# Layer norm of the next element: its sums by accumulating transfers instead of matmuls, and begun one stage earlier

## The chip, the cores and the metric

The kernel runs on one core of a Trainium2 chip. The metric is the device time of one execution in microseconds (us). One execution was also taken by the hardware profiler; its trace gives start and duration of every instruction, and tells for each idle stretch of an engine what ended it. The engines are TensorE (PE in the profile; PEld is its weight load), VectorE (DVE), ScalarE (ACT), GpSimd (POOL) and SyncE (SP). Here POOL and SP mostly issue transfers (DMAs). A time such as 1149.31 is us from the start of the span.

## The reference

Two layers are applied to x of 8 elements, 512 channels and 32 x 32 positions (1024 tokens), all in float32. Layer 0 normalises each token over its channels, runs attention with eight heads of 64 channels, projects, and adds its input. Layer 1 normalises groups of 16 channels, runs attention with one head over all 512 channels, projects, and adds its input.

```
# layer 0, S = 1024 tokens, C = 512
mu = mean(x_flat, axis=-1);  var = mean((x_flat - mu)**2, axis=-1)
xn = (x_flat - mu) * rsqrt(var + 1e-5) * gamma + beta
q, k, v = xn @ Wq.T + bq, xn @ Wk.T + bk, xn @ Wv.T + bv      # 8 heads
out = softmax(q k^T / 8) v;   x1 = out @ Wo.T + bo + x_flat
# layer 1
h = group_norm(x1, 32 groups)
q, k, v = wq h + bq, wk h + bk, wv h + bv
o = softmax(q^T k / sqrt(512)) v;   y = x1 + wp o + bp
```

## The kernel before, in words

x is kept with channels on the partitions. A block `x_b_jk` (128 x 1024 numbers) holds 256 channels j of 512 tokens k, as two chunks of 128 channels side by side; four blocks are one element. The projections and layer 1's two large products are done by the class `Product`: 2 x 2 blocks with seven block products instead of eight. Each product is one `step`, and `STEPS` names which of three PSUM tiles x, y and z it writes. After a step ScalarE copies a PSUM tile away (`copy`) or VectorE adds such a copy and another PSUM tile to make an output (`out`, line 343). A later step that writes the same PSUM tile waits for this. A unit is seven steps, and there are two or four units to a project.

The program goes through the elements in order. For element b the stages are: values and queries of layer 0 (`v`, `q`), eight pairs of heads (`Pair`: scores at line 683, exponential at 686, values at 701), keys of element b+1, output project and group norm, then layer 1: `qa`, scores `s1`, values `vm`, and the last product `o1` (`Whole.values`), whose outputs y are scaled by the inverse of the sums (line 905), get a bias and layer 1's input (line 906) and are stored (line 907). The input of layer 1 was put away in DRAM (`x1_away`) and comes back as `x1r` (line 904), one load to an output. After `o1` come values and queries of element b+1, and in them the layer norm of element b+2. The four blocks of x for it are loaded there.

The instructions of TensorE, VectorE, ScalarE and POOL stand in the order in which the program makes them (`manual_schedule`). Small pieces of other work wait in the list `side`. `tick`, called in each step between the matmuls and the copy, takes the next piece (two where `pieces` is 2) and puts its instructions there. An engine works through its list in order, so an instruction that waits holds all behind it. SyncE's loads and stores are not in this written order: a scheduler places them by when it believes them ready. On SyncE's queue too a transfer that waits, for instance a store whose output isn't there, holds those behind it.

The layer norm of the next element is such a chain of pieces (`LayerNorm.steps`), queued after the third step of the first `v` unit (`LN_AT`). VectorE adds the four channel chunks of x (lines 524 and 528, tile `lns`). TensorE adds over the 128 partitions with a matrix of 1/512 (line 519): the mean, to PSUM, two matmuls for the two halves of the tokens, each of which the trace records as two. ScalarE copies the mean to both halves of the partitions (line 537), VectorE centres x (543), ScalarE squares it (547), the squares are added (tile `lnq`) and summed over partitions by TensorE in the same way. `root` takes the variance from PSUM with a transpose (491), makes its inverse root, copies it to the partitions and expands it (496); then x is scaled (571) and gets gamma and beta (575).

The sums of the exponentials take another way already. `halve` is an accumulating transfer on POOL's queue that adds the upper 64 partitions of a tile to the lower ones; `fold` adds the remaining two times 32 partitions and lays half a row of tokens on each group of 32 partitions of a small tile; VectorE transposes and reduces this (lines 720, 721). So a sum over partitions is made without TensorE. Groups of two pairs are folded together (`PairSums`), after the values of the first of them. Layer 1's sums go the same way in `Whole.fold`, and `Whole.inverse` uses them during the second step of `o1`; ScalarE spreads the inverse with eight small copies (878) and VectorE expands it.

Of the kernel before, what the change touches and what calls it, by code (L numbers as in the profile page):

```python
# [19 lines left out]
P = 128  # L20
EPS = 1e-5
NUM_GROUPS = 32
HEADS = 8
LN_AT = 3

# [41 lines left out]
def fast_path(ctx: ExitStack, tc: tile.TileContext, x: bass.AP, vecs: dict, weights: dict, out: bass.AP,  # L67
# [244 lines left out]
    def later(*work):  # L312
        side.extend(work)
# [180 lines left out]
    def expand(t, r):  # L494

        nc.vector.transpose(t.rearrange("p (k i) -> p k i", i=BL), r.unsqueeze(2).to_broadcast((P, r.shape[1], BL)))  # L496

    def inverse_root(r, var, name):

        t = small.tile(list(r.shape), F32, tag=f"{name}_t", name=f"{name}_t")  # L500
        nc.scalar.activation(t, var, AF.Ln, bias=eps)
        nc.scalar.activation(r, t, AF.Exp, scale=-0.5)

        def refine():
            nc.vector.scalar_tensor_tensor(t, var, EPS, r, ALU.add, ALU.mult)
            nc.vector.scalar_tensor_tensor(t, t, -0.5, r, ALU.mult, ALU.mult)
            nc.vector.scalar_tensor_tensor(r, t, 1.5, r, ALU.add, ALU.mult)
        return refine

    class LayerNorm:  # L510


        def __init__(self, b, xt):
            self.b, self.xt = b, xt

# [15 lines left out]
        def mean(self):  # L531
            ps = bank(f"mean_{self.b}")
            self.over_channels(ps)
            self.mu = big_tile(f"mu_{self.b}")
            for k in range(NH):
                for r in range(2):
                    nc.scalar.copy(self.mu[ts(r, D), ts(k, HB)], ps[ts(k, D), :])

        def rows(self, t, k):
# [37 lines left out]
        def steps(self):  # L577

            self.sq = {}
            for k in range(NH):  # L580
                yield from self.add("lns", k, self.xt[0, k], self.xt[1, k])
            yield
            self.mean()
            yield
            yield
            blocks = ((0, 0), (1, 0), (0, 1), (1, 1))
# [9 lines left out]
            yield from self.add("lnq", 1, self.sq[0, 1], self.sq[1, 1])  # L596
            yield
            self.variance()
            yield
            yield from self.root()  # L600
            for n in range(4):
# [107 lines left out]

    def fold(f, q, t, cols):  # L710

        for n in range(2):
            nc.gpsimd.dma_start(out=f[ts(q, BL), :], in_=t[ts(n, BL), cols], accum_op=ALU.add if n else ALU.bypass)  # L713

    def halve(t):
        nc.gpsimd.dma_start(out=t[:D, :], in_=t[D:, :], accum_op=ALU.add)  # L716

    def folded_sums(d, t, f):

        nc.vector.transpose(t, f)  # L720
        nc.vector.tensor_reduce(d, t.rearrange("p (k i) -> p k i", i=BL), mybir.AxisListType.X, ALU.add)

    class PairSums:


        def __init__(self, two):
            self.two, self.tag = two, two[0].tag
            self.r = small.tile([P, HB // BL], F32, tag="r", name=f"r_{self.tag}")
            self.rr = [small.tile([P, HB // BL], F32, tag=f"rr{n}", name=f"rr_{p.tag}") for n, p in enumerate(two)]

        def fold(self):

            self.f = half_tile(f"fold_{self.tag}")
            for pair in self.two:
                halve(pair.sum)
            for n, pair in enumerate(self.two):
                for i in range(2):
                    fold(self.f, 2 * n + i, pair.sum, ts(i, HB))

# [53 lines left out]
    class Whole:  # L793
# [61 lines left out]
        def fold(self):  # L855
            self.f = half_tile(f"fold1_{self.b}")
            for hf in range(NH):
                halve(self.total[hf])
            for a in range(2):
                for hf in range(NH):  # L860
                    fold(self.f, 2 * a + hf, self.total[hf], ts(a, HB))

        def inverse(self):
# [4 lines left out]
            def invert():  # L868
                d = small.tile([P, HB // BL], F32, tag="d", name=f"d1_{b}")
                folded_sums(d, half_tile(f"fold1t_{b}"), self.f)  # L870
                nc.vector.tensor_copy(both[:D, :], d[D:, :])
                nc.vector.tensor_add(both[:D, :], both[:D, :], d[:D, :])
                invert_sums(r[:D, :], both[:D, :])
# [60 lines left out]
    with tc.manual_schedule(engines=ORDERED):  # L934
        nq = natural(wq, "q1")
        nk = natural(wk, "k1")
        ln = LayerNorm(0, x_next)
        pieces = ln.steps()
# [36 lines left out]
        for n, w in (("v", wv_now), ("q", wq_now), ("o", wo), ("a", wa), ("m", wm)):  # L975
            complete_later(n, w)
        later(*(lambda c=c: score_bias(c) for c in range(NC)))
        units, kt = project("k0", wk_now, bias_of("bk0"), hb)
        for u in units:
# [3 lines left out]

        def next_values_and_queries(b, wv, wq):

            xt = load_x(b + 1) if b + 1 < B else None
            units, v = project_v(f"v{b}", wv, hb)
            units[0].step(LN_AT)
            ln = None
            if xt:  # L990
                ln = LayerNorm(b + 1, xt)
                ln.queue()
# [3 lines left out]
            for u in units:  # L996
                u.pieces = 2
            units[0].rest()
            return ln, v, q, units[1]

        ln, vts, qt, q_last = next_values_and_queries(0, wv_now, wq_now)
        for b in range(B):
            more = b + 1 < B
            stats = small.tile([P, NC, NH, 6], F32, tag="stats", name=f"stats_{b}")
            ot = {"tag": f"o_{b}"}
            first = Pair(b, 0, 0, qt, kt, vts, ot)
            first.scores(range(NM))
            q_last.rest()
            pairs = [first] + [Pair(b, hf, c, qt, kt, vts, ot) for hf in range(NH) for c in range(NC) if hf + c > 0]
            for i, p in enumerate(pairs):  # L1010
                if i + 1 < len(pairs):
                    pairs[i + 1].scores(range(NM))
                if i < 2 and more:
# [6 lines left out]
                if i == 7 and more:  # L1020
                    hb = operands(ln.result())
                    add_operands(hb)
                p.values(scaled=(p is pairs[-1]))
                if i % 2 == 0:
                    sums = PairSums(pairs[i : i + 2])
                    if i + 2 < len(pairs):
                        sums.fold()
                    else:
                        sums.product()
                        later(sums.invert, sums.copies, lambda: sums.rows(1), lambda: sums.rows(0),  # L1030
                              lambda: sums.scale(0))
                elif i + 1 < len(pairs):
                    at_scores.append(sums.invert_folded)
# [49 lines left out]
            if more:  # L1083
                wv_next, wq_next = load_w("v", b + 1), load_w("q", b + 1)
            o_units = whole.values(vm)
            check = iter(()) if more else all_checks()
            o_units[0].step(1)
            whole.inverse()
            o_units[0].step(1)
            next(check, None)  # L1090
            o_units[1].step(2)
            next(check, None)
            for u in o_units:
                u.rest()
            until(lambda: not side)
            if more:
                kt = {ik: block(f"k{b + 1}_again_{ik[0]}{ik[1]}") for ik in kn_away}
                for ik, d in kn_away.items():
                    nc.sync.dma_start(out=wide(kt[ik]), in_=d)
                ln, vts, qt, q_last = next_values_and_queries(b + 1, wv_next, wq_next)  # L1100

# [383 lines left out]
```

## Time and profile before

Three runs took 2935.98, 2937.20 and 2937.74 us, median 2937.2.

| what | us |
|---|---|
| the profiled execution's own time | 2937.39 |
| its span, first to last instruction | 2935.6 |
| TensorE busy | 2914.7 |
| VectorE busy | 1788.5 |
| ScalarE busy | 1044.1 |
| POOL busy | 238.5 |
| share of TensorE in the chain that ended last | 98% |
| granted clock of TensorE, mean | 0.997 |
| busy share of the 16 DMA engines, queue of SyncE | 20.4% |
| the same, queue of POOL | 7.7% |

A group's row gives line, engine and operation, the tiles it writes and reads, shapes and count, then busy time, mean ns of one, and the engine's idle time before it with what ended it. In a timeline a row is: start, us, engine, line, operation, tiles, shapes, count, and idle time before in brackets. Rows of one tile overlap on TensorE, since a matmul starts before the one before has ended; what an instruction costs there is the distance of the starts. A row of transfers ends with the size of one and the median us from issue to landing.

One element takes 358.3 us from its mark to the next one's. In the element that the prediction follows, layer 1's last product `o1` runs from 1104.62 to 1152.69, the values of the next element to 1178.07, its queries to about 1191.6.

### The profile page before, as it was taken

How to read it: one execution, taken by the hardware profiler on the slowest of the kernel's cores; microseconds unless marked ns; L12 is line 12 of the kernel's file. 1: busy time of each engine (PE TensorE's matmuls, PEld its weight loads, DVE VectorE, ACT ScalarE, POOL GpSimd, SP SyncE). 2: the span in 40 equal slices, each digit the busy share in tenths (PEclk: the TensorE clock that was granted, in tenths of full speed). 3: DMA queues.
4: the chain of work that ended last, by engine and by line, in shares of the span. 5: the costliest groups of instructions: out<-in, count | busy, mean ns of one | idle time of the engine just before them, and what ended most of it. 6: DMA issues, size and time to landing. Idle time of an engine off the chain costs nothing.

```text
span 2935.6 us, 26956 instructions
## 1 busy us (share of the span) xinstructions
PE 2914.7 (99%) x9787; PEld 1374.3 (47%) x9787; DVE 1788.5 (61%) x2298; ACT 1044.1 (36%) x1641; POOL 238.5 (8%) x357
## 2 busy tenths in 40 slices
PE   9999999999999999999999999999999999999998
PEld 4534455345543455434553345533455334553344
DVE  6677456774567654675557765577555675537744
ACT  3462215612156121651216512264223632226221
POOL 2020000200011000110001100011000100002000
PEclk9999999999999999999999999999999999999999
DMA  8124141231312323132232322322231231412302
GB/s 296 59 47 146 53 136 35 58 138 55 125 39 55 136 66 113 43 83 104 69 111 47 83 101 77 103 52 78 100 112 68 58 107 65 122 33 63 109 4 70
DMA packets 100286, 250.93 MB, mean 85 GB/s; under 512 B 13824, under 2 KB 17968, under 8 KB 100144
## 3 DMA queue, kind: packets, MB, share of 16 engines
q1 hardware_dynamic: 81616, 204.51, 20.4%
q0 software_dynamic: 18432, 44.59, 7.7%
q8 instruction: 79, 1.29, 0.2%
q14 instruction: 63, 0.52, 0.1%
q10 hardware_dynamic: 96, 0.02, 0.0%
HBM read 156.26 MB, written 59.24 MB: 73 GB/s over the span
## 4 chain that ended last, share of the span: by engine, by line
PE 98%; DVE 1%; DMA 0%; issue 0%; ACT 0%; SPq 0%; DVEq 0%
PE s L683 15%; PE acc L701 15%; PE x_o L429 6%; PE x_s L421 6%; PE y_s L421 4%; PE y_o L429 4%; PE z_s L421 4%; PE z_o L429 4%; PE x_q L404 3%; PE x_k L404 3%; PE x_qa L404 3%; PE x_v L413 3%; PE x_vm L413 3%; PE x_out L404 3%; PE y_q L404 2%; PE z_qa L404 2%
## 5 line engine op out<-in xcount | busy, mean ns | idle before, releaser
L686 ACT ACTIVATE p<-s 128x1024 f32<-128x1024 f32 x512 | 476.4, 1050 | 77.3 <-PE s L683 77.2
L692 DVE TENSOR_TENSOR sum<-sum,p 128x1024 f32<-128x1024 f32 x384 | 470.3, 1225 | 38.9 <-ACT p L686 0.9
L701 PE MATMUL acc<-p,v 128*64 128x512 f32 x2048 | 453.6, 595 | 0.0
L683 PE MATMUL s<-q,k_again 64*128 64x512 f32 x1792 | 399.9, 596 | 0.0
L701 PEld LDWEIGHTS acc<-p,v 128*64 128x64 f32 x2048 | 141.4, 137 | 305.0 <-issue 292.2
L683 PEld LDWEIGHTS s<-q,k_again 64*128 64x128 f32 x1792 | 166.3, 185 | 232.0 <-issue 116.1
L716 POOL DMA_DIRECT2D sum<-sum x64 | 54.9, 859 | 2294.9 <-PE z_vm L413 1139.3
L713 POOL DMA_DIRECT2D fold<-sum x256 | 171.2, 764 | 292.5 <-DMA fold<-sum 281.6
L690 DVE TENSOR_TENSOR sum<-p,p 128x1024 f32<-128x1024 f32 x64 | 78.4, 1225 | 190.0 <-ACT p L686 190.0
L421 PE MATMUL x_s<-S_qa,T_gn 128*128 128x512 f32 x256 | 120.3, 592 | 0.0
L429 PE MATMUL x_o<-T_p,S_vm 128*128 128x512 f32 x256 | 115.2, 592 | 0.0
L822 ACT ACTIVATE p<-p 128x512 f32<-128x512 f32 x128 | 80.7, 630 | 73.1 <-DVE p L343 73.1
L705 ACT COPY o<-acc 128x512 f32<-128x512 f32 x56 | 32.8, 586 | 197.4 <-PE acc L701 197.4
L343 DVE TENSOR_TENSOR p<-u(1, 1)_s,y_s 128x512 f32<-128x512 f32 x32 | 22.0, 689 | 132.3 <-ACT u(1, 1)_s L434 132.3
L451 ACT ACTIVATE u(0, 0)_k<-x_k,vecs 128x512 f32<-128x512 f32 x16 | 11.0, 687 | 239.7 <-PE x_k L404 211.0
L343 DVE TENSOR_TENSOR y<-u(1, 1)_o,y_o 128x512 f32<-128x512 f32 x16 | 11.0, 688 | 134.7 <-ACT u(1, 1)_o L434 134.7
L421 PEld LDWEIGHTS x_s<-S_qa,T_gn 128*128 128x128 f32 x256 | 48.6, 190 | 61.2 <-issue 61.0
L429 PEld LDWEIGHTS x_o<-T_p,S_vm 128*128 128x128 f32 x256 | 48.6, 190 | 60.7 <-issue 60.7
L758 ACT COPY rr<-r 32x16 f32<-32x16 f32 x256 | 51.6, 202 | 58.2 <-DVE r L657 55.3
L496 DVE STREAM_TRANSPOSE rden<-rr 128x512 f32<-128x512 f32 (+1 forms) x72 | 51.5, 750 | 26.1 <-ACT rr L878 13.4
L343 DVE TENSOR_TENSOR qa<-u(1, 1)_qa,y_qa 128x512 f32<-128x512 f32 x16 | 11.0, 687 | 82.4 <-ACT u(1, 1)_qa L451 82.4
L413 PE MATMUL x_vm<-w_m,T_gn 128*128 128x256 f32 x256 | 60.5, 379 | 0.0
(327 smaller groups left out, 4541.8 us busy)
## 6 DMA issues: line engine op xcount, KB each, us to landing
x<-in_x_dram SPq DMA_DIRECT2D x32, 512.0 KB, 6.0
sum<-sum POOLq DMA_DIRECT2D x64, 256.0 KB, 3.5
fold<-sum POOLq DMA_DIRECT2D x256, 64.0 KB, 2.4
xr<-in_x_dram SPq DMA_DIRECT2D x64, 256.0 KB, 6.8
x_away<-x SPq DMA_DIRECT2D x32, 512.0 KB
x1r<-x_away SPq DMA_DIRECT2D x64, 256.0 KB, 5.9
out_dram<-y SPq DMA_DIRECT2D x64, 256.0 KB, 2.5
k_away<-k SPq DMA_DIRECT2D x28, 512.0 KB, 2.6
```

The source lines that it names most:

```text
L404: nc.tensor.matmul(dst, a[:, k, ts(r, P)], b[:, k, :], start=(opens and k == 0), stop=(k == 1), skip_group_check=True)
L413: nc.tensor.matmul(dst[:, ts(m, CB)], b[:, k, ts(2 * r + m, P)], a[:, k, :], start=(opens and m == 0 and k == 0), stop=(k == 1), skip_grou ...
L421: nc.tensor.matmul(dst, b[:, k, ts(r, P)], a[:, k, :], start=(opens and k == 0), stop=(k == 1), skip_group_check=True)
L429: nc.tensor.matmul(dst, a[:, m, ts(r, P)], b[m // 2][:, m % 2, :], start=(opens and m == 0), stop=(m == NM // 2 - 1), skip_group_check=True)
L683: nc.tensor.matmul(s[:, ts(i, HB)], self.k[m // 4][r, ts(m % 4, P)], self.q[r, :], start=True, stop=True)
L686: nc.scalar.activation(p, s, AF.Exp, scale=1.0 / float(D) ** 0.5)
L690: nc.vector.tensor_add(self.sum, self.p[0], p)
L692: nc.vector.tensor_add(self.sum, self.sum, p)
L701: nc.tensor.matmul(acc[i * D : (i + 1) * D, :], value_of(self.vt, m, self.c * P + i * D, D), self.p[m][:, ts(i, HB)], start=(m == 0), stop ...
L713: nc.gpsimd.dma_start(out=f[ts(q, BL), :], in_=t[ts(n, BL), cols], accum_op=ALU.add if n else ALU.bypass)
L716: nc.gpsimd.dma_start(out=t[:D, :], in_=t[D:, :], accum_op=ALU.add)
L822: nc.scalar.activation(dest(i, k), dest(i, k), AF.Exp, scale=float(C) ** -0.5)
```

## The change

For elements 2 to 7 (`folded`) the layer norm is made without matmuls, and begun one stage earlier.

- `sums` puts four transfers on POOL's queue after the first step of `o1`: the four channel chunks of x, from DRAM, to one tile, the last three accumulating. `fold("mu")` follows: a halving and four folds.
- x itself is loaded, and the pieces queued, when the first unit of `o1` is done. The first piece is `folded_means`: transpose, reduce, scaling by 1/512 on VectorE, then eight small copies on ScalarE (`spread`); the second expands the mean on VectorE. Centring, squares and their sums follow in the steps of the second `o1` unit and of the values.
- The sum of squares is folded by a halving and four folds. Then the pieces pass without work (`waiting`) until the first step of the queries, and `root_folded` goes on from the folded sums.
- `fold` now makes both plain copies before both accumulating ones. Each pair's sum is halved and folded right after its scores (`PairSums.take`).
- `w_q` is loaded after `o1` in the program, not at its start. In SyncE's placed order the loads of x come right after the first store of `o1`, where k_again and x were mixed before. The last two x1r loads of `o1` now stand behind the stores of the outputs before them, with two loads of `w_q` between; the rest of `w_q` and all of `k_again` follow.
- In the queries one piece is taken in each step for all elements but 0, where it was two.
- `Whole.inverse` adds the folded halves by two copies and two sums of 32 partitions instead of one of each of 64.

```diff
+        def sums(self):
+
+            self.total = big_tile(f"lns_{self.b}")
+            for c in range(NC):
+                nc.gpsimd.dma_start(out=self.total, in_=x[self.b, ts(c, P), :],
+                                    accum_op=ALU.add if c else ALU.bypass)
+            self.fold("mu")
...
+        def fold(self, name):
+            self.f = half_tile(f"fold_{name}_{self.b}")
+            halve(self.total)
+            fold(self.f, 0, self.total)
+
+        def folded_means(self, name):
+
+            d = small.tile([P, HB // BL], F32, tag=f"ln{name}", name=f"ln{name}_{self.b}")
+            t = half_tile(f"fold{name}_{self.b}")
+            folded_sums(d[:D, :], t[:D, :], self.f[:D, :])
+            nc.vector.tensor_scalar(d[:D, :], d[:D, :], 1.0 / C, None, ALU.mult)
+            return d
+
+        def spread(self, name, r):
+            rr = small.tile([P, NH, HB // BL], F32, tag=f"ln{name}r", name=f"ln{name}r_{self.b}")
+            for j in range(4):
+                for k in range(NH):
+                    nc.scalar.copy(rr[ts(j, BL), k, :], r[ts(k, BL), :])
+            yield
+            t = big_tile(f"{name}_{self.b}")
+            setattr(self, name, t)
+            expand(t, rr.rearrange("p k i -> p (k i)"))
+            yield
...
         def steps(self):
 
             self.sq = {}
-            for k in range(NH):
-                yield from self.add("lns", k, self.xt[0, k], self.xt[1, k])
-            yield
-            self.mean()
-            yield
-            yield
+            if self.folded:
+                yield from self.spread("mu", self.folded_means("m"))
+            else:
+                for k in range(NH):
+                    yield from self.add("lns", k, self.xt[0, k], self.xt[1, k])
+                yield
+                self.mean()
+                yield
+                yield
...
-            yield
-            self.variance()
-            yield
-            yield from self.root()
+            if self.folded:
+                self.fold("var")
+                yield
+                while self.waiting:
+                    yield
+                yield from self.root_folded()
+            else:
+                yield
+                self.variance()
+                yield
+                yield from self.root()
...
+    def fold(f, q, t):
+
+        for n in range(2):
+            for i in range(NH):
+                nc.gpsimd.dma_start(out=f[ts(q + i, BL), :], in_=t[ts(n, BL), ts(i, HB)],
+                                    accum_op=ALU.add if n else ALU.bypass)
...
             if more:
-                wv_next, wq_next = load_w("v", b + 1), load_w("q", b + 1)
+                wv_next = load_w("v", b + 1)
             o_units = whole.values(vm)
...
             o_units[0].step(1)
+            ln = LayerNorm(b + 2) if b + 2 < B else None
+            if ln:
+                ln.sums()
             whole.inverse()
             o_units[0].step(1)
...
             o_units[1].step(2)
...
-            for u in o_units:
-                u.rest()
-            until(lambda: not side)
+            o_units[0].rest()
+            if ln:
+                ln.xt = load_x(b + 2)
+                ln.queue()
+            o_units[1].rest()
+            if more:
+                wq_next = load_w("q", b + 1)
```

## The prediction

> **What bounds the kernel now.** I read the page's busy times and chain first: they say which engine's work sets the end.
>
> ```profile
> span 2935.6 us, 26956 instructions
> PE 2914.7 (99%) x9787; PEld 1374.3 (47%) x9787; DVE 1788.5 (61%) x2298; ACT 1044.1 (36%) x1641; POOL 238.5 (8%) x357
> PE 98%; DVE 1%; DMA 0%; issue 0%; ACT 0%; SPq 0%; DVEq 0%
> ```
>
> TensorE works 99% of the span and is 98% of the chain. So an edit is worth the TensorE time that it removes, less each wait that it creates in front of a matmul. Nothing else counts. Next the view of line 519, the matmuls that the change removes, and TensorE's timeline around them, for the element that I follow throughout (layer norm of element 4, which in the changed kernel runs beside the end of element 2 and the values of element 3):
>
> ```profile
> L519 PE MATMUL mean<-lns,ones_c x32: 592/618/643, 19.4 to 2243.8; 128*64 128x512 f32 x32
> L519 PE MATMUL var<-lnq,ones_c x32: 592/643/1116, 32.3 to 2260.5; 128*64 128x512 f32 x32
> ...
> 1161.32 1.89 PE L413 MATMUL z_v<-w_v,T_h 128*128 128x256 f32 x8
> ...
> 1166.50 1.89 PE L413 MATMUL z_v<-w_v,x 128*128 128x256 f32 x8
> 1168.32 1.08 PE L519 MATMUL mean<-lns,ones_c 128*64 128x512 f32 x4
> 1169.33 1.99 PE L413 MATMUL x_v<-w_v,T_h 128*128 128x256 f32 x8
> 1171.16 1.89 PE L413 MATMUL y_v<-w_v,T_h 128*128 128x256 f32 x8
> ```
>
> Durations overlap, so I price by starts. A step of the values project takes 1.726 us from start to start. From 1166.50 to 1171.16 two steps pass, 3.45 us, but 4.66 us go by: the mean costs 1.21 us, its slower neighbours included. The variance, four records between two steps of the queries, costs the same by the same reading (1183.22 to 1187.86 is 4.64 us, two steps of 1.717 are 3.43): 1.21 us.
>
> **What is removed.** 2.41 us for each of elements 2 to 7: 6 x 2.41 = 14.5 us. The built program of the changed kernel has 24 TensorE matmuls fewer (48 records) and the rest in the old order, so this part is certain. Elements 0 and 1 keep theirs.
>
> **What takes its place, and where it hides.**
>
> *The sums by transfers.* Fourteen more transfers per element on POOL's queue: four of 512 KB (x from DRAM, the last three accumulating), a halving, four folds; then a halving and four folds for the variance. No row accumulates 512 KB. The nearest:
>
> ```profile
> sum<-sum POOLq DMA_DIRECT2D x64, 256.0 KB, 3.5
> fold<-sum POOLq DMA_DIRECT2D x256, 64.0 KB, 2.4
> ```
>
> 192 KB more cost 1.1 us, so 512 KB accumulating take about 3.5 + 1.5 = 5.0 us (estimate), a plain one 3.9 (the row of w_o). [...] Each link waits for the one before: 3.9 + 3 x 5.0 + 3.5 + two rounds of folds (2.9 each) = 28 us. In the old kernel POOL issues layer 1's last fold at 1102.13; the x sums stand behind these folds in its queue. The changed order of the folds can only bring that forward. So the folded mean lands by about 1131. [...] VectorE reaches it only behind unit 0's last output, whose add with x1r now ends at 1137.9: 7 us to spare. [...] The trace has a DMA share of 0.48 over 1104.5 to 1152.6, so I let every link's data time (2.6 us of the 5.0) stretch by half: 1136, still in time. If this cover goes, the price is one for one: VectorE's wait holds ScalarE's eight small copies of the mean, these hold the copy of x_o queued behind them, and the second next step of layer 1's values waits for that copy.
>
> *Even in time, that place is tight.* Transpose, reduce and scaling take 1.7 us (0.70, 0.69, 0.17 and starts), ScalarE's eight copies 1.69 (row of L878), the copy of x_o 0.59: done at 1142.0; TensorE wants it at 1142.4. Cost 0, up to 0.3 if it slips.
>
> *The variance's folds* are issued when lnq is ready, near 1166, and land about 10 us later at 1176; VectorE asks at about 1178. The square root's ScalarE work is as before. Cost 0. Layer 1's inverse has two more VectorE operations of 0.17 us; the output behind them ended at 1113.5 and its bank is wanted at 1114.9. Cost 0. The pairs' folds now start one pair's scores earlier: cost 0, no gain, since nobody waited for them.
>
> *SyncE's queue, the step that costs.* It is reordered. The loads of w_q (1.75 MB) and k_again (2 MB) move behind layer 1's last outputs; needed at 1178 and after 1190, they come in time. But they now stand between the last x1r loads. Before:
>
> ```profile
> 1148.91 0.34 SPq L907 DMA_DIRECT2D out_dram<-y  x1
> 1149.31 0.42 SPq L904 DMA_DIRECT2D x1r<-x_away  x1
> 1151.69 3.77 SPq L907 DMA_DIRECT2D out_dram<-y  x2
> ...
> 1152.89 0.69 DVE L343 TENSOR_TENSOR y<-u(0, 1)_o,y_o 128x512 f32<-128x512 f32 x1 [1.23 <-PE y_o L429]
> 1153.61 0.69 DVE L905 TENSOR_TENSOR y<-y,rden 128x512 f32<-128x512 f32 x1
> 1154.34 0.75 DVE L906 SCALAR_TENSOR_TENSOR y<-y,bm,x1r 128x512 f32<-128x512 f32 x1
> ```
>
> The last x1r was issued at 1149.31 and landed 3.2 us later, in time for 1154.34. In the changed order 1149.31 carries the last but one, then two loads of w_q (1 MB); the store behind them waits for the output that needs that x1r (it lands at 1152.5, its add ends at 1153.3); and only then, at 1153.7, comes the last x1r. When does it land? Store and x1r alone took 3.6 us. A burst of 2 MB of the same kinds (store, x1r, three k_again) took from 1115.01 to 1124.8, another from 1473.55 to 1481.7: 1.5 MB more cost 4.6 to 6.2 us. Here, too, 1.5 MB follow the first half megabyte: 1148.91 + 3.6 + (4.6 to 6.2) = 1157.1 to 1158.7, middle 1157.9.
>
> Who waits: VectorE's final add of layer 1 (y with x1r), and in order behind it the centring of x (1.22, starts 1.13 apart), the first sum of squares (1.22), the output v(0,0) (0.69), two more sums (0.69, 1.22) and the output v(1,1) (0.69). From the add's start to v(1,1)'s end that is 0.67 + 1.13 + 1.13 + 0.60 + 0.60 + 1.13 + 0.69 = 5.95 us. TensorE needs v(1,1) for the step at 1163.05. So the add must start by 1157.0; landing at 1157.9 starts it at 1158.0: 1.0 us lost per element, 0.2 to 1.8 by the two bursts. The old kernel had none of this layer-norm work in front of v(0,0).
>
> *Does a short stall also slow the clock?* [...] waits of 3 us twice near 2775 bring the granted clock to 0.51 over 2780 to 2786. [...] I add nothing. [...]
>
> *The engines' totals* hardly move. Per element VectorE loses two wide sums (1.22), two half ones (0.69), four copies (0.18) and a transpose (0.72), and gains the folds' two transposes and reduces (0.70 each), two scalings (0.17) and the mean's expansion (1.25); ScalarE swaps 2.37 us of copies for two times 1.69. Only their places matter, as told.
>
> **The sum.** (2.41 - 1.0) x 6 = 8.5 us. The profiled execution took 2937.39 us with a span of 2935.6, 1.8 us around it that stay; it stands 0.2 above the median of 2937.2. So the span should become 2927.1, the time 2928.7.
>
> **Rivals.** (a) The last x1r is in time, because the DMA engines move its queue at the better rate or v's chain is shorter than I add up: all 14.5 us arrive, 2922.7. For it: DMA share 0.06 in the values stage, and with nothing ahead the last x1r would land at 1156.9, just at the limit. Against it: the 1 MB of w_q ahead. (b) The wait eats the gain: landing at 1159.2 costs 2.3 us per element: 2936.5. For it: x1r rows up to 9.2 us from issue to landing. (c) Slower: the accumulating chain is late. Its three 512 KB links have 7 us to spare, so it decides from 7.3 us a link on (half as much again as my 5.0), and breaks even with the removed matmuls at 8.1. At 9 us a link the mean lands at 1143, TensorE stands 5 us per element, 30 us in all: 2952.7. For it: x comes from DRAM while SyncE's transfers run. Against it: links start from a safe bound, and 256 KB need 3.5. (d) That the matmuls are not removed is excluded by the built program.
>
> **Chances.** A residue of 0.2 to 1.4 us per element, 0.44, time 2924 to 2931, likeliest 2928.7; (a) 0.30; (b) and its neighbours with 1.4 to 3.4 us lost, 0.19; (c) or more lost, 0.07. This kernel's measurement tells 0.2% (5.9 us) from no change: faster is below 2931.3, which is the first two cases, 0.74; within it 0.19; slower 0.07. Range 2922 to 2936: it takes in (a) and most of (b).
>
> **What would show it.** The mean and variance rows: 8 records each instead of 32. VectorE's add with x1r waiting for "DMA x1r" near 1158 (less 2.4 to 5 us by then), and a gap of some 1 us in TensorE before z_v or y_v in unit 0 of each element's values, and nowhere else. The fold of the mean landing 5 to 10 us before its transpose starts. Wrong if the transpose waits for the fold, if the gap stands before x_o, if the granted clock falls at these places, or if there is no gap.

## The result and the profile after

The changed kernel takes 2924.78 us (median, 2923.55 to 2928.49); the kernel before, run beside it, took 2936.59. The ratio is 0.9962, with a 95% interval of 0.9944 to 0.9979: 11.8 us gained, where the forecast was 8.5 of the 14.5 removed. Its profiled execution took 2924.38 us with a span of 2922.7.

First the page's busy times and chain, then the view of the line that makes means and variances on TensorE, now line 542:

```profile
PE 2899.4 (99%) x9739; PEld 1371.7 (47%) x9739; DVE 1784.9 (61%) x2302; ACT 1048.9 (36%) x1713; POOL 303.8 (10%) x441
PE 96%; DVE 2%; DMA 1%; issue 0%; ACT 0%; SPq 0%; DVEq 0%; ACTq 0%
```

```profile
L542 PE MATMUL mean<-lns,ones_c x8: 592/618/643, 19.3 to 92.2; 128*64 128x512 f32 x8
L542 PE MATMUL var<-lnq,ones_c x8: 592/618/643, 32.4 to 109.0; 128*64 128x512 f32 x8
```

The two rows end at 92 and 109 us: from element 2 on there are no such matmuls. TensorE still sets the end. VectorE and DMA, which had 1% and 0% of the chain, have 2% and 1%: new waits lie on it. VectorE's timeline at the end of layer 1's last product, in the element that the prediction follows, shows them:

```profile
1147.42 0.75 DVE L963 SCALAR_TENSOR_TENSOR y<-y,bm,x1r 128x512 f32<-128x512 f32 x1 [0.82 <-DMA x1r<-x_away]
1148.09 1.22 DVE L599 TENSOR_TENSOR x<-x,mu 128x1024 f32<-128x1024 f32 x1
...
1152.48 0.75 DVE L963 SCALAR_TENSOR_TENSOR y<-y,bm,x1r 128x512 f32<-128x512 f32 x1 [1.85 <-DMA x1r<-x_away]
1153.15 1.22 DVE L599 TENSOR_TENSOR x<-x,mu 128x1024 f32<-128x1024 f32 x1
1154.29 1.22 DVE L547 TENSOR_TENSOR lnq<-sq,sq 128x1024 f32<-128x1024 f32 x1
1155.42 0.68 DVE L342 TENSOR_TENSOR v<-u(0, 0)_v,z_v 128x512 f32<-128x512 f32 x1
...
1157.76 0.68 DVE L342 TENSOR_TENSOR v<-u(1, 1)_v,y_v 128x512 f32<-128x512 f32 x1
```

The last add with x1r waits 1.85 us for its load; the layer norm's work follows, and only then the outputs of the values. TensorE's timeline beside it, and behind it the place where the mean's matmuls stood:

```profile
1154.89 1.89 PE L412 MATMUL x_v<-w_v,T_h 128*128 128x256 f32 x8
1156.62 1.89 PE L412 MATMUL z_v<-w_v,T_h 128*128 128x256 f32 x8
1158.49 1.99 PE L412 MATMUL y_v<-w_v,x 128*128 128x256 f32 x8
1160.32 1.89 PE L412 MATMUL x_v<-w_v,x 128*128 128x256 f32 x8
1162.05 1.89 PE L412 MATMUL z_v<-w_v,x 128*128 128x256 f32 x8
...
1165.50 1.89 PE L412 MATMUL y_v<-w_v,T_h 128*128 128x256 f32 x8
```

Two steps from 1156.62 to 1160.32 take 3.70 us instead of 3.45: this element lost 0.25 us here. From 1162.05 to 1165.50 two steps take 3.45 us, where they took 4.66 with the mean between them.

Lining up all of TensorE's starts of the two traces gives a ledger of the span.

- The twelve places of removed matmuls, 1.21 us each: 14.5 gained.
- The two steps behind the variance's place, which were slower too in the old kernel (1187.86 to 1189.66 is 1.80 us, not 1.72): 0.8 gained.
- y_v and z_v in the values' first unit, and the x_v just behind: 2.8 lost, 0.2 to 1.2 per element.
- y_out, in the output project, which waits for other loads and differs between executions of one kernel: 1.3 lost.
- The first 100 us: 1.4 gained, which is luck. TensorE pauses for 1.5 us near 34 us in both traces. In the old one its clock is then 0.53 over 34.5 to 38.0, in the new one 1.00.
- The last stages: 0.7 gained.

Together this is 13.3, and the spans differ by 12.9.

### The profile page after: what moved, and what is told of

It reads as the page before. It is cut to its first block, busy times and chain, and to the rows that moved or that the text cites. A ratio compares the mean times of both kernels' runs of the same rounds, so it can differ in the third digit from the quotient of the medians.

```text
span 2922.7 us, 27038 instructions
## 1 busy us (share of the span) xinstructions
PE 2899.4 (99%) x9739; PEld 1371.7 (47%) x9739; DVE 1784.9 (61%) x2302; ACT 1048.9 (36%) x1713; POOL 303.8 (10%) x441
## 4 chain that ended last, share of the span: by engine, by line
PE 96%; DVE 2%; DMA 1%; issue 0%; ACT 0%; SPq 0%; DVEq 0%; ACTq 0%
PE s L749 15%; PE acc L767 15%; PE x_o L428 6%; PE x_s L420 6%; PE y_s L420 4%; PE z_s L420 4%; PE y_o L428 4%; PE z_o L428 4%; PE x_k L403 3%; PE x_qa L403 3%; PE x_q L403 3%; PE x_vm L412 3%; PE x_v L412 2%; PE x_out L403 2%; PE y_k L403 2%; PE y_q L403 2%
## 5 line engine op out<-in xcount | busy, mean ns | idle before, releaser
L963 DVE SCALAR_TENSOR_TENSOR y<-y,bm,x1r 128x512 f32<-128x512 f32 x64 | 48.1, 752 | 59.3 <-DMA x1r<-x_away 57.9
```

## Experiments

Two theories were set against each other. A: what is lost is lost to the last x1r of layer 1, which lands late. B: the layer norm's own work on VectorE, now in front of the values' outputs, is too long for that place whenever x1r comes. A third question was how near the chain of accumulating transfers comes to its consumer. All these runs are edits of the changed kernel; their ratios are to the kernel before, run beside them.

**The changed kernel again** (`again`), timed beside `x1r_ahead`, `link_more` and `link_less`:

> The changed kernel once more, beside the others on one chip. Theory A (the residue is the late last x1r load): 2924.8, with short gaps before y_v in the first values unit of each element again, some 2.7 us in all. Theory B (the residue is the layer-norm work itself in VectorE's queue there): the same.

2925.80 us (2924.49 to 2928.93), 2936.33 before; ratio 0.9965, interval 0.9953 to 0.9978. The pauses at y_v, z_v and x_v come to 3.9 us here, and the last add of the followed element waited 2.69 us for x1r where it had waited 1.85. So the loss scatters between executions: 0.46 and 0.65 us per element on average.

**The last x1r one output earlier** (`x1r_ahead`): all work and all orders of TensorE and VectorE stay; each of the last two loads is issued with the output before its own.

```diff
+                xrs = {}
+                def load(i, k):
+                    xrs[i, k] = half_tile(f"x1r_{b}_{k}_{2 * i + r}")
+                    nc.sync.dma_start(out=xrs[i, k], in_=self.x1[i, k][:, ts(r, HB)])
...
-                    xr = half_tile(f"x1r_{b}_{k}_{oc}")
-                    nc.sync.dma_start(out=xr, in_=self.x1[i, k][:, ts(r, HB)])
+                    if (i, k) not in xrs:
+                        load(i, k)
+                    xr = xrs[i, k]
+                    if (i, k) == (1, 1):
+                        load(1, 0)
+                    elif (i, k) == (1, 0):
+                        load(0, 1)
```

> Each last x1r load of a unit is issued one output earlier, ahead of the store and of w_q; nothing else changes. Theory A: VectorE no longer waits for x1r at the last output, the add starts some 1 us before the limit, the gaps before y_v (2.7 us over six elements) are gone, the time is 2922. Theory B: the wait goes, the gaps stay, the time stays 2924.8.

2921.42 us (2920.00 to 2921.99); ratio 0.9948, interval 0.9934 to 0.9961: 4.4 us under `again`, whose pauses came to 3.9. VectorE's timeline of this kernel, the same two adds and the output v(1,1):

```profile
1146.79 0.75 DVE L974 SCALAR_TENSOR_TENSOR y<-y,bm,x1r 128x512 f32<-128x512 f32 x1
...
1150.04 0.75 DVE L974 SCALAR_TENSOR_TENSOR y<-y,bm,x1r 128x512 f32<-128x512 f32 x1
...
1157.65 0.69 DVE L342 TENSOR_TENSOR v<-u(1, 1)_v,y_v 128x512 f32<-128x512 f32 x1 [1.33 <-ACT u(1, 1)_v L433]
```

Neither add waits. The last one starts 2.4 us earlier, and v(1,1) then waits for TensorE's product by way of ScalarE, not TensorE for v(1,1). The pauses at y_v, z_v and x_v are gone in every element. VectorE did the same layer-norm work in the same order, so B falls and A is shown: the work has room there if its start isn't held up.

**Which part of the queue makes it late?** SyncE's timeline of the changed kernel, around the last two x1r loads:

```profile
1144.17 0.33 SPq L964 DMA_DIRECT2D out_dram<-y  x1
1144.60 0.38 SPq L961 DMA_DIRECT2D x1r<-x_away  x1
1145.07 0.86 SPq L203 DMA_DIRECT2D w_q<-saved_q  x2
1148.20 0.34 SPq L964 DMA_DIRECT2D out_dram<-y  x1
1148.58 0.42 SPq L961 DMA_DIRECT2D x1r<-x_away  x1
1149.10 0.90 SPq L203 DMA_DIRECT2D w_q<-saved_q  x2
```

The last x1r (1148.58) stands behind a store (1148.20), which waits for an output (its add ends at 1148.17), and behind the 1 MB of w_q issued at 1145.07. `loads_late` takes the loads away and leaves the stores; `wq_old` puts w_q back to the start of `o1` and so lets two loads of k_again (also 1 MB) move up.

```diff
...
+            if late:
+                units[0].step(3)
+                wq = late()
...
-            if more:
-                wq_next = load_w("q", b + 1)
...
+                def late():
+                    w = load_w("q", b + 1)
+                    for ik, d in kn_away.items():
+                        kt[ik] = block(f"k{b + 1}_again_{ik[0]}{ik[1]}")
+                        nc.sync.dma_start(out=wide(kt[ik]), in_=d)
+                    return w
...
```

> The loads of w_q and of the kept keys are emitted only after three steps of layer 1's values, so that SyncE's queue has nothing but stores of outputs ahead of the last x1r loads, which keep their places behind those stores. If the megabyte of w_q ahead of the last x1r makes it late, it now lands some 2.5 us after its issue instead of 3.9, VectorE's last add with x1r waits about 0.5 us instead of 1.9, the gaps before y_v and z_v in the first values unit shrink from about 0.5 us to at most 0.15 per element, and the time is 2922 to 2923.5, most of what the earlier issue of the loads brought (2921.4). If it is late only because it is issued behind the store of an output, the gaps stay and the time is 2925 to 2926.

```diff
-                wv_next = load_w("v", b + 1)
+                wv_next, wq_next = load_w("v", b + 1), load_w("q", b + 1)
...
-            if more:
-                wq_next = load_w("q", b + 1)
```

> The load of w_q goes back to the place that it had before the change (with w_v, before layer 1's outputs); two of the four loads of the kept keys, 1 MB as well, then stand ahead of the last x1r. If what counts is how many bytes stand ahead, gaps and time stay as in the changed kernel: 2925 to 2926, some 0.5 us per element before y_v or z_v. If it is w_q's own transfers, the gaps go and the time is about 2922.

`loads_late` took 2921.84 us (2920.33 to 2924.13), ratio 0.9950, interval 0.9937 to 0.9964; `wq_old` 2925.61 us (2923.78 to 2928.44), ratio 0.9966, interval 0.9954 to 0.9978. Before, beside them, 2936.30. SyncE's and VectorE's timelines of `loads_late`, then the same of `wq_old`:

```profile
1149.78 0.42 SPq L961 DMA_DIRECT2D x1r<-x_away  x1
1153.79 0.33 SPq L964 DMA_DIRECT2D out_dram<-y  x1
1154.17 1.93 SPq L203 DMA_DIRECT2D w_q<-saved_q  x4
```

```profile
1153.01 0.75 DVE L963 SCALAR_TENSOR_TENSOR y<-y,bm,x1r 128x512 f32<-128x512 f32 x1 [1.18 <-DMA x1r<-x_away]
1158.70 0.69 DVE L342 TENSOR_TENSOR v<-u(1, 1)_v,y_v 128x512 f32<-128x512 f32 x1 [0.33 <-ACT u(1, 1)_v L433]
```

```profile
1144.57 0.87 SPq L1169 DMA_DIRECT2D k_again<-k_away  x2
1148.24 0.43 SPq L961 DMA_DIRECT2D x1r<-x_away  x1
```

```profile
1152.50 0.75 DVE L963 SCALAR_TENSOR_TENSOR y<-y,bm,x1r 128x512 f32<-128x512 f32 x1 [2.21 <-DMA x1r<-x_away]
```

With nothing but the store ahead, the last x1r lands 3.2 us after its issue in this element (1149.78 to 1153.01; 2.5 was expected), and 2.8 to 3.2 in the six, 2.9 on average. With 1 MB of w_q ahead it took 3.9 us here (1148.58 to 1152.48), in `again` 4.7, and with 1 MB of k_again ahead (`wq_old`) 4.3; the averages over six elements are 4.0, 4.0 and 4.0. So it does not matter whose bytes they are.

`loads_late` also took away the loads that follow the last x1r, so no run separates the bytes ahead of it from those behind. The packets of SyncE's queue in the changed kernel do, in the followed element. This is their row (packets, MB, busy share) from the start of this group of transfers, just before 1145, to the issue of the last x1r (window 1144.95 to 1148.58):

```profile
q1 hardware_dynamic: 446, 1.11, 93.2%
```

Of the 1.84 MB issued ahead (two stores, an x1r, two loads of w_q) 1.11 had moved, so 0.73 MB were still to come: the last store's 0.26 and 0.46 that `loads_late` does not have. When x1r landed, the same row for 1144.95 to 1152.4 says 2.26 MB, 0.16 more than all up to x1r itself (2.10). So most of the delay is bytes ahead.

The add still waits 1.18 us in `loads_late` (I had expected 0.5), because it is still issued behind a store; but v(1,1) is now in time, waiting 0.33 us for the product, and all pauses at y_v, z_v and x_v are gone. So the store's share of the wait is hidden, and the loads' share, 1.1 us on average, was the whole loss. The profiled execution of `loads_late` was the slowest of its five (2924.13); the records behind the 1.5 us pause near 34 us are slow in it, as in the kernel before (991 and 1015 ns apart instead of 522 and 534).

One reading sums this up. Line up each trace with the kernel before at the first matmul of the values, and see how much later than there (1154.34 in the followed element) the last add starts. There are 42 such places in the traces of `after` (the changed kernel), `again`, `x1r_ahead`, `loads_late`, `wq_old`, `pairs_old` and `link_less`. In 14 of them, the twelve of `x1r_ahead` and `loads_late` among these, it starts at most 2.60 us later and TensorE loses nothing. In the other 28 it starts 2.76 to 4.31 us later, and TensorE loses 0.16 to 1.71 us, each time that delay less 2.60, to within 0.02. The prediction's limit, 1157.0, lies 2.66 us behind 1154.34. Nothing but the late start is needed to account for this loss.

**How near is the chain of transfers?** One more link of 512 KB for the mean (`link_more`: chunk 0 is loaded twice, the second plain copy replacing the first, so the sum is the same), and one less (`link_less`: the sum leaves out the last 128 channels, so the mean is one of 384 channels).

```diff
-            for c in range(NC):
+            for n, c in enumerate([0, *range(NC)]):
...
-                                    accum_op=ALU.add if c else ALU.bypass)
+                                    accum_op=ALU.add if n > 1 else ALU.bypass)
```

> The first chunk of x is copied twice in the chain of sums, the second copy behind the first: one link of 4.2 us more per element. The folded mean landed 0.2 to 2.9 us (mean 1.5) before its transpose. If the chain has only this to spare, and 0.4 us behind it, TensorE loses about 2.3 us per element before x_o of layer 1's values: 14 us, 2939. If VectorE has slack elsewhere, or the chain has the 7 us that the prediction gave it: 2925.

```diff
-            for c in range(NC):
+            for c in range(NC - 1):
```

> The last chunk of x is left out of the mean's sum (so the mean is of 384 of the 512 channels): one accumulating link of 5.6 us less per element. If the chain is hidden, as the prediction has it: 2924.8, no change beyond 1 us. If its lateness is what leaves the residue: 2922.

`link_more` took 2940.15 us (2935.25 to 2945.42), ratio 1.0012, interval 1.0003 to 1.0020: 14 us over `again`, and slower than before. `link_less` took 2924.04 us (2923.11 to 2926.32), ratio 0.9956, interval 0.9941 to 0.9972: like the changed kernel. In `link_less` the folded mean lands 6.6 to 7.5 us before its transpose, and still the pauses at y_v, z_v and x_v come to 4.8 us: the chain is not what leaves that loss. The view of the folded mean's transposes in `link_more` says who waits (us, times); the VectorE and TensorE timelines at the worst element say how long; and the row of a stretch, whose last three columns are granted clock, DMA share and GB/s, what came behind:

```profile
  DMA fold_mu<-lns: 14.2, 6
```

```profile
782.01 0.70 DVE L509 STREAM_TRANSPOSE foldm<-fold_mu 64x512 f32<-64x512 f32 x1 [4.60 <-DMA fold_mu<-lns]
```

```profile
786.02 6.28 PE L428 MATMUL x_o<-T_p,S_vm 128*128 128x512 f32 x8 [3.99 <-ACT u(0, 1)_o L433]
792.14 3.60 PE L428 MATMUL z_o<-T_p,vm 128*128 128x512 f32 x8
```

```profile
784.00:790.00 6.00, 3.98 (x5) 1.85 (x6) 2.47 (x2) 1.88 (x8) 0.00 (x0) 0.53 0.00 0
```

All six transposes wait, 14.2 us together, and TensorE waits in front of x_o for the copy (785.39) behind ScalarE's eight (783.66, 1.70 us), as the prediction had named it. At 786.02 the step of eight records takes 6.1 us to the next start instead of 3.4: after a pause of 3.99 us the clock is at 0.53 over 784 to 790. TensorE's loss in front of x_o is 16.3 us in this trace, 11.9 of them pauses and 4.5 slow clock. So the extra link reaches TensorE as 2.0 us of pauses per element, and more again where they are long: the chain is hidden in the changed kernel, but by little.

**The pairs' folds at their old place** (`pairs_old`):

```diff
-                if n == 0:
-                    self.f = half_tile(f"fold_{self.tag}")
-                halve(pair.sum)
-                fold(self.f, 2 * n, pair.sum)
...
+        def fold(self):
+            self.f = half_tile(f"fold_{self.tag}")
+            for pair in self.two:
+                halve(pair.sum)
+            for n, pair in enumerate(self.two):
+                fold(self.f, 2 * n, pair.sum)
...
+                if i % 2 == 0 and sums.folded:
+                    sums.fold()
```

> The halvings and folds of layer 0's pairs go back to their old place, one pair's scores later; all else is as in the changed kernel. If their earlier place neither gains nor costs, as forecast, the time is that of the changed kernel within its scatter, 2924.5 to 2926.5. If they now hold up the queue of POOL ahead of the sums of x, the folded mean lands later, stalls appear before x_o at the end of layer 1, and the time is 2928 or more. If their earlier place gained something, the time is 2927 or more without such stalls.

2924.52 us (2921.63 to 2927.83); ratio 0.9958, interval 0.9945 to 0.9972. No difference from the changed kernel, in either direction; the pauses at y_v, z_v and x_v come to 4.4 us in its trace, and none stands before x_o, though two of the six transposes wait 0.1 and 0.2 us for their folds.

**Element 1 as well.** The change folds elements 2 to 7 alone. Would element 1 bring 2.4 us more, on top of `x1r_ahead`?

```diff
-        ln = LayerNorm(1, False)
+        ln = LayerNorm(1)
+        ln.sums()
```

> The last x1r loads are issued one output earlier, and the layer norm of element 1 is folded as well, its sums of x issued before element 0's layer 1. If each folded layer norm is worth the 2.41 us of TensorE that its mean and variance take, and the chain of element 1's sums is early there, the time is 2921.4 - 2.4 = 2919.0. If the chain of sums holds up something at the start of element 0's values, it is 2921 or more, with a gap there.

It took 2930.52 us (2929.38 to 2932.76), ratio 0.9982, interval 0.9974 to 0.9989: 9 us more than `x1r_ahead`, not 2.4 less. VectorE's and TensorE's timelines in element 0's queries:

```profile
110.85 0.70 DVE L509 STREAM_TRANSPOSE foldv<-fold_var 64x512 f32<-64x512 f32 x1 [9.52 <-DMA fold_var<-lnq]
```

```profile
105.50 1.88 PE L403 MATMUL y_q<-T_h,w_q_first 128*128 128x512 f32 x4
116.16 3.48 PE L403 MATMUL x_q<-T_h,w_q_first 128*128 128x512 f32 x4 [8.78 <-ACT u(0, 1)_q L450]
```

The mean's chain was early there, and its place gained 1.2 us. But lnq is only ready at 100.7, as the queries begin, and the variance's folds land 10.1 us later, at 110.8, while VectorE asks for them at 101.3. TensorE stands 8.8 us, and its next step then takes 3.32 us to the next start (116.16 to 119.48) instead of 1.72. Two more runs moved that question back, from one step of the queries' first unit to seven (`best_later`; that is all of the unit's steps, which its expectation counted as eight) and to five (`best_mid`).

```diff
-            units[0].step(1)
+            units[0].step(1 if b else 7)
```

> As the run named best, but the layer norm of element 1 asks for the variance's folds six steps of the queries later (10.3 us), after seven of the eight steps of their first unit instead of one. If the 7.8 us stall and the 2 us of slow clock in best came from VectorE waiting 9.5 us for these folds in front of the queries' outputs, both go, and the time is 2921.4 - 2.4 = 2919.0, the best of all. If the folded layer norm of element 1 costs elsewhere, 2922 or more.

```diff
-            units[0].step(1)
+            units[0].step(1 if b else 5)
```

> As best_later, but the layer norm of element 1 asks for the variance's folds after five of the seven steps of the queries' first unit: by the trace of best_later the folds have landed there, and the eight sums of the first scores do not yet stand on VectorE ahead of the square root's small operations. If the 4.3 us stall and the slow clock after it in best_later came from those small operations standing behind the scores' sums, both go, and the time is 2919 to 2920. If ScalarE's eight small copies of the inverse root now hold the scores' exponentials, a new gap stands in or behind the first scores and the time is 2921 or more.

`best_later` took 2923.73 us (2922.36 to 2924.54; before beside it 2935.81), `best_mid` 2922.99 us (2921.95 to 2924.30; before 2935.58); ratios 0.9957 (0.9944 to 0.9971) and 0.9959 (0.9946 to 0.9973). TensorE's timelines, first `best_later`, then `best_mid`:

```profile
128.12 3.09 PE L403 MATMUL x_q<-T_h,w_q_first 128*128 128x512 f32 x4 [4.32 <-ACT u(0, 0)_q L450]
```

```profile
117.48 6.26 PE L749 MATMUL s<-q,k 64*128 64x512 f32 x20 [1.99 <-ACT p L752]
```

In the one, VectorE's transpose of the folds (125.29) stands behind the first scores' sums (7.87 us from 117.51), and the copy of the next unit behind it. In the other the folds have landed almost in time (VectorE waits 0.32 us), but ScalarE's eight copies (114.68, 1.70 us) now hold the first exponentials (116.40), the rival that its expectation named. With the slow records behind them (the clock is 0.95 over 126 to 160 in `best_later`, 0.66 over 117 to 122 in `best_mid`) the pauses cost 6.3 and 4.8 us against the starts of `x1r_ahead`, more than the 2.5 that the removed matmuls bring in these traces. Three places were tried for element 1 and none gains; others were not tried. By its time alone `best_mid` is not clearly slower than `x1r_ahead`: the intervals of the two ratios overlap. `x1r_ahead` stays the fastest, 2921.42 us, below both kernels.

## Why the prediction was right, and where its sizes were off

*Removal, 2.41 us per element.* Right, and a little small: in the changed trace the starts close up by 1.21 us at each of the twelve places, and by 0.13 more in the two steps behind each variance, whose slowness the price left out.

*SyncE's queue, 1.0 us lost per element.* Right in mechanism and place; the term was mis-sized: 0.46 us per element in this trace (2.8 us in six), 0.65 in `again`. The add was to start at 1158.0 on the clock of the kernel before. It started at 1152.48, and TensorE is 4.70 us ahead up to there, which makes 1157.18: 0.2 us behind the limit of 1157.0, and 0.25 us were lost. Two sizes did this. The load before it landed 2.8 us after its issue, not 3.2, so the store and the last x1r went out 0.4 us earlier than I had it (1153.3 on the old clock, not 1153.7). And the last x1r took 3.9 us where the mean of my two bursts said 4.2. The chain on VectorE from the add's start to the start of v(1,1) was forecast as 5.26 us and is 5.28. The forecast of 2928.7 is high by 3.9 us, of which this term is 3.2 (6.0 - 2.8); another 0.6 is that the kernel before took 2936.59 in this comparison and 2937.2 in the runs forecast from. That these two make up nearly all of it is partly luck: the other terms of the ledger, put at nothing, scatter by 1 or 2 us from one execution to the next. Two interventions on the cause, `x1r_ahead` and `loads_late`, remove the pauses, as rival (a) has them removed, and come to within 1.3 us of that rival's 2922.7.

*The sums by transfers.* The conclusion (cost 0) held, the reasons only in part. Rows of transfers, with the median from issue to landing:

```profile
lns<-in_x_dram POOLq DMA_DIRECT2D x24, 512.0 KB, 5.3
lns<-lns POOLq DMA_DIRECT2D x6, 256.0 KB, 7.4
fold_mu<-lns POOLq DMA_DIRECT2D x24, 64.0 KB, 3.1
lnq<-lnq POOLq DMA_DIRECT2D x6, 256.0 KB, 3.6
```

The link was estimated at 5.0 us and takes 5.3: the row of 256 KB was the right base. But the halving was put at 3.5 and takes 7.4; the same halving for the variance takes 3.6. POOL's timeline, and SyncE's for the same stretch, show what ran beside it:

```profile
1109.42 0.87 POOL L535 DMA_DIRECT2D lns<-in_x_dram  x1 [4.89 <-DMA lns<-in_x_dram]
1115.13 0.82 POOL L505 DMA_DIRECT2D lns<-lns  x1 [4.85 <-DMA lns<-in_x_dram]
1124.12 1.05 POOL L501 DMA_DIRECT2D fold_mu<-lns  x2 [8.17 <-issue]
1128.55 1.61 POOL L501 DMA_DIRECT2D fold_mu<-lns  x2 [3.38 <-DMA fold_mu<-lns]
```

```profile
1111.02 2.31 SPq L149 DMA_DIRECT2D x<-in_x_dram  x2
1113.42 0.48 SPq L961 DMA_DIRECT2D x1r<-x_away  x1
1113.99 1.31 SPq L149 DMA_DIRECT2D x<-in_x_dram  x2
1121.21 0.36 SPq L964 DMA_DIRECT2D out_dram<-y  x1
1121.62 1.02 SPq L961 DMA_DIRECT2D x1r<-x_away  x2
```

SyncE issues 2.25 MB of x and x1r just before the halving, and two more x1r during it; from the halving's issue to that of its folds 9.0 us pass (1115.13 to 1124.12). In `link_more`, where the extra link puts the halving behind these loads, the same row falls to a median of 4.1 us, and the last link, which now meets them, takes 9.2 to 10.4 us. In `link_less`, where the halving comes ahead of them, 4.2 us pass from its issue to that of its folds in the followed element (1109.55 to 1113.78), and the folds behind it rise to a median of 5.2 us instead. So in these three traces whichever transfer meets the loads is the slow one; the loads themselves were not moved in any run. I had let every link's data time stretch evenly by half, my estimate from the DMA share of 0.48; the delay fell on the halving, which took twice its time, and on the folds (3.1 us against the 2.4 of the old row). The whole chain lasts 39 us (1093.91 to 1132.92), not 28 or 33. It came out even because it began earlier than I bounded it: at 1093.91, which is 1098.6 on the old clock, 3.5 us ahead of the old last fold. The folded mean then landed at 1137.6 on the old clock, where I had 1131, or 1136 with that stretch, and 1137.9 as the last moment. That the cost still came out at 0 is luck. The spare time was forecast as 7 us, or 2 with it. Landing against transpose in the six elements, it is 2.9, 1.5, 0.2, 2.0, 1.1 and 1.3 us, 1.5 on average; in `x1r_ahead` one of the six transposes waited 0.3 us. So "landing 5 to 10 us before its transpose" was wrong. `link_more` shows what the thin cover means: the forecast's price, one for one, held for the pauses (14.2 us of waits on VectorE, 11.9 on TensorE, with some 0.4 us of room per element), and the slow clock (0.53 over 784 to 790) came on top.

*That place tight, cost 0.* Right: mean, copies and the copy of x_o are in time; no pause stands before x_o in the changed kernel. *Variance's folds, layer 1's inverse, pairs' folds, cost 0.* Right: in no element does VectorE wait for fold_var; the pairs' place was tried alone and makes no difference.

*A short stall does not slow the clock.* Right for what occurred: behind the pauses in the values, up to 0.6 us at one step in the changed kernel and 0.9 in all these runs, the records follow at their usual distance from the second on; in the followed element the clock is 1.00 over 1152 to 1163. But that they would was my estimate, and nothing cited for it showed it. The waits that I cited near 2775 are 2.37, 0.84 and 2.62 us, with two short matmuls between each, not 3 us twice. And the kernel's own trace before had a pause of 1.48 us, at 34.86, with the clock at 0.53 over 34.5 to 38.0 behind it, which the prediction overlooked (below).

*Rivals.* (a), all of the gain, did not happen by itself but is what `x1r_ahead` makes of the change. (b) fell: the largest loss of one element was 1.2 us, 1.7 in `again`, and not 2.3 in each. (c) fell for the change but its mechanism is real: it was put to decide from 7.3 us a link, 2.3 us over each of three; with 1.5 us to spare and links of 5.3 it decides from about 5.8, and one extra link turned the gain into a loss.

## What to carry to other kernels

When a load is moved to make room on a queue, look at which small load then stands behind it and who needs that one: here 1 MB of weights, first used some 25 us later, stood ahead of one 256 KB tile and cost 3 to 4 us of 14.5, and issuing the small load one output earlier gave them back. Work out the limit first, by adding up what stands on the waiting engine between the small load and the bounding engine's need: here that sum was right to 0.1 us, and the late load cost exactly what it was late beyond it. A chain of dependent transfers was not priced here by its rows in a quiet stretch (a halving of 3.5 us took 7.4): lay the other queues' transfers beside it in time, and find which link they fall on. And work that is taken off the bounding engine has to be asked for late enough; for element 1 the same trade lost more in pauses than it gained at each of three places.

## What was not expected of the hardware

Whether a pause of TensorE slowed its clock was not settled by its length here. The same pause stands near 34 us in all twelve traces, 1.46 to 1.50 us long, where the variance of the first layer norm waits for VectorE. These are the rows before and after the change:

```profile
34.86 1.97 PE L519 MATMUL var<-lnq,ones_c 128*64 128x512 f32 x2 [1.48 <-DVE lnq L528]
34.98 1.07 PE L542 MATMUL var<-lnq,ones_c 128*64 128x512 f32 x2 [1.50 <-DVE lnq L551]
```

In four traces (the kernel before, `x1r_ahead`, `loads_late`, `pairs_old`) the next records are slow, two of them 991 and 1015 ns apart instead of 522 and 534, and some 1.6 us are lost; the clock of the kernel before is 0.53 over 34.5 to 38.0, that of `x1r_ahead` 0.96 over 0 to 40. In the other eight nothing is lost: the clock of the changed kernel is 1.00 over 34.5 to 38.0, that of `best_later` 1.00 over 0 to 40. Later in the kernel longer pauses were followed by slow records. Behind 3.99 us (`link_more`, at 786.02) the clock is 0.53 over 784 to 790. Behind 4.32 us (`best_later`, at 128.12) two steps take 2.88 and 2.35 us to the next start instead of 1.72, and the clock is 0.95 over 126 to 160. Behind 8.78 us (`best`, at 116.16) a step takes 3.32 us instead of 1.72. One of 1.99 us (`best_mid`, at 117.48) was followed by slow records too: the clock is 0.66 over 117 to 122, and 1.7 us more are lost. Why the same pause of 1.5 us goes both ways was not shown. By these runs a pause of 1.5 to 2 us cost its length alone (1.50 in the changed kernel) or about twice that (1.48 and some 1.6 more before, 1.99 and 1.7 more in `best_mid`).

An accumulating transfer within one tile of 256 KB took 3.4 to 3.6 us in quiet stretches and a median of 7.4 us beside SyncE's loads. The 512 KB loads from DRAM, all but the first of a chain accumulating, have a median of 5.3 us, but the last of each chain, where it met those loads, took up to 8.4 us, and up to 10.4 in `link_more`.
